# Four attention layers on one core: inputs turned by VectorE in blocks of 32, sums of exponentials on VectorE beside one layer, and both ends of a side layer placed last

## The chip, the cores and the metric

The kernel runs on one core of a Trainium2 chip. The metric is the device time of one execution in microseconds (us). The time before is the median of three runs. One more execution was taken by the hardware profiler, and all durations of single instructions come from that one.

The engines are called TensorE (PE in the profile, with its weight loads as PEld), VectorE (DVE), ScalarE (ACT), GpSimd (POOL) and SyncE (SP), which issues most DMAs.

## What is computed

The input x has 4 elements of 64x64 positions with 64 channels in float32. Four attention layers follow one another; every element goes through them alone. Cut to what matters:

```python
# layer 0: attention over all 4096 positions, normalised over j, summed over the queries
q, k, v = x @ Wq + bq, x @ Wk + bk, x @ Wv + bv          # each 4096 x 64
attn = softmax(q @ k.T, axis=-1)
x = gamma * (attn.T @ v) + x
# layer 1: 4096 queries with 8 channels, 1024 pooled keys, values with 32 channels
attn = softmax(theta(x) @ maxpool2(phi(x)).T)
x = x + sigma * ((attn @ maxpool2(g(x))) @ w_o + b_o)
# layers 2 and 3: group norm, then attention over all 4096 positions, projection, residual
w = softmax(q @ k.T / 8);  x = residual + (w @ v) @ Wp + bp
```

In layer 0 the factor 1/sum belongs to the row of the score matrix, and the rows are what the second product sums over. So the sum of a row's exponentials is needed before that product, and it is applied to the values.

## The kernel before, in words

**Stages and steps.** The fast path runs 12 attention stages one after another: layer 0 of elements 0 to 3 and layers 2 and 3 of each, mixed so that the small work between them always has a stage to run beside. A stage has 64 steps. `step` puts out, in this order, the two score tiles of the step with their exponentials (`first`, twice), and then the second products of an earlier step (`due`). The order of instructions on every engine is the order in which the Python code emits them; each engine works through its own list in order and waits on semaphores.

**Layer 0** (`layer0`). `first` writes a scores tile `s` of 128x1024 by four matmuls (L971), takes the exponential into a tile `p` (L975) and has ScalarE's accumulator sum each row into a column of `zs`. Every fourth tile completes a row block: VectorE adds the four columns (L977) and takes the reciprocal (L978). Three steps later `scale` multiplies the values by it on ScalarE (L985, `vs`), and `adds` forms the second product (L996).

**Layers 2 and 3** (`attention`). Scores are L1214, exponentials L1219, second products L1249. The sums are kept by VectorE, which adds every `p` to `zacc` (L1225).

**Tiles.** There are two scores tiles in PSUM, and everything that writes PSUM for a moment takes them in turn: scores, transposes, projections, sums. A matmul that needs one waits until the engine that read its last content is done. Accumulators have four tiles of their own. In SBUF there are 14 tiles for `p`.

**Side work.** `background` holds a generator, a chain of small pieces: layer 1 of an element, and what must be done before its next layer. Each `yield` names the place in a step where the next piece may go:
- MID: between the two second products of a step.
- ALONE: as MID, and no LATE piece in that step.
- LATE: in the middle of the second of these products.
- END: after all else.

A step grants pieces by a credit (`tempo`: 1.0 beside most of layer 0, 3.0 beside the stages that carry layer 1).

**Layer 1** (`layer1`). It runs as side work, over two halves j of the queries and 8 blocks k of the keys each. LATE gives two scores tiles (L1089) and their exponentials (L1095). VectorE adds these up (`accumulate`, L1104). With `bank` the second product stays in an accumulator; that is so for elements 1 to 3, beside layer 2. For element 0, beside layer 0 of element 1, there is no free accumulator (`bank` false): each second product (L1115, at END) goes to a scores tile, and VectorE adds it to `o` (L1124), the first one of each half being copied by ScalarE (L1126). `finish(j)` ends a half: row sums by TensorE (L1131), copied and summed by ScalarE (L1137), four reciprocals (L1140), a product (L1142), another sum on ScalarE for the range check (L1144), the output projection (L1150) and the addition to x (L1152). The end of half 0 is put between the scores of half 1, that of half 1 comes last.

**Inputs.** `load_x` loads an element in 8 DMAs of 32 partitions, each with pieces of 64 channels (256 bytes), positions on partitions. `transposed` turns it to channels on partitions: for each half, 8 TensorE transposes (L916) into a scores tile, copied out by VectorE (L862) or ScalarE (L870). This is the beginning of `before0`, which goes on with the projection (L883) and the values (L902, L903). Element 0 is loaded and transposed ahead of the first stage; elements 1, 2 and 3 as side work of stages 1, 3 and 5. Only element 1's copies are on VectorE.

**The end.** A flag, `bad`, counts partitions whose sums are out of range (L1776). After the last DMAs (L1516), all engines load it (L1793) and branch (L1794) around `general_path`, a slower form of the computation that is not run with these inputs.

Of the kernel before, what the change touches and what calls it, by code (L numbers as in the profile page):

```python
# [10 lines left out]
AF = mybir.ActivationFunctionType  # L11
ALU = mybir.AluOpType
AX = mybir.AxisListType
# [581 lines left out]
            layer3(layer2(layer1(layer0(here))), dst)  # L595


def fast_path(tc: tile.TileContext, a: dict, out: bass.AP, bad):

# [6 lines left out]
    nc = tc.nc  # L608
    x = a["x"]
# [162 lines left out]
    now = [0]  # L772
    due, before, urgent = {}, {}, []
    later = []
    back = {"gen": iter(()), "at": None, "credit": 0.0, "tempo": 1.0, "alone": -1}

    def background(tempo, *phases):
# [131 lines left out]
    def transposed(on, st):  # L909
        xin = st.pop("xin")  # L910
        xT = st["x"] = x_tile("xT")
        for g in range(2):
# [3 lines left out]
                nc.tensor.transpose(bank[i // 4][:, ds(i % 4 * P, P)], xin[:, g * 8 + i, :, :].rearrange("p i c -> p (i c)"), ident)  # L916
            evacuate(on, xT[:, wide(g)], s)

    def before0(on, st):
        yield from transposed(on, st)  # L920
        q = x_tile("q")
        yield from project(on, q, blocks[0][0], st["x"], blocks[0][1])
        st["q"] = q, swapped("q_swapped", q)
        st["v"] = x_tile("v").rearrange("p (j f) -> p j f", f=C)
        yield from values(st["v"], wv0, st["x"], bv0)
# [23 lines left out]
    def layer0(st):  # L949

        q, k, v = st.pop("q"), st["x"], st.pop("v")
        pairs = NB * NC // 2
        acc, ps, zs, scaled = {}, {}, {}, {}
        zsum, rz = check_columns(NB)

        def queries(m, i, e):

            c, n = divmod(m // 2, 4)
            return q[(c + i) % 2][half(i), ds(c // 2 * 1024 + m % 2 * 512 + n * P + e * C, C)]

        def first(u):
            m, c = divmod(u, NC)
            if c == 0:
                zs[m] = small.tile([P, NC], FP, tag="z0", name="z0")
            s = s_tile()
            for i in range(2):
                for e in range(2):  # L970
                    nc.tensor.matmul(  # L971
                        s[half(e), chunk(i)], queries(m, i, e), k[half(i), chunk(c)], start=True, stop=True
                    )
            p = ps[u] = p_tile()
            nc.scalar.activation(p, s, AF.Exp, accum_out=zs[m][:, c : c + 1])  # L975
            if c == NC - 1:
                nc.vector.tensor_reduce(zsum[:, m : m + 1], zs.pop(m), AX.X, ALU.add)  # L977
                nc.vector.reciprocal(rz[:, m : m + 1], zsum[:, m : m + 1])  # L978

        def scale(t):  # L980
            vs = scaled[t] = z_p.tile([P, C], FP, tag="vs", name="vs", bufs=1)
            for e in range(2):
                if 0 <= t - e < pairs:
                    m = 2 * (t - e) // NC
                    nc.scalar.activation(  # L985
                        vs[half(e), :], v[half(e), m, :], AF.Copy, scale=rz[half(e), m : m + 1]
                    )

        def add(t, e, n, vs, cols):

            if 0 <= t < pairs:
                m, c = divmod(2 * t + n, NC)
                if m == 0 and e == 0 and c not in acc:
                    acc[c] = acc_tile()
                for i in range(2):
                    nc.tensor.matmul(  # L996
                        acc[c][half(i), cols], vs[half(e), :], ps[2 * t + n][half(e), chunk(i)][:, cols],
                        start=(m == 0 and e == 0), stop=(m == NB - 1 and e == 1),
                    )
                    yield  # L1000

        def adds(t, n, within=None):
            for cols in parts(within, t * 2 < NC or t >= pairs - NC // 2):
                lower, upper = add(t, 0, n, scaled[t], cols), add(t - 1, 1, n, scaled[t], cols)
                for row_tile in (lower, upper) * 3:
                    next(row_tile, None)
            if n == 1:
                del scaled[t]
                for u in (2 * t - 2, 2 * t - 1):
                    ps.pop(u, None)  # L1010

        def finish(cs):
            xT = st["x"]
            for c in cs:
                nc.vector.scalar_tensor_tensor(xT[:, chunk(c)], acc.pop(c), gamma0, xT[:, chunk(c)], ALU.mult, ALU.add)
            if not acc:
                st["done0"] = True

        start = now[0]
        for t in range(pairs + 1):  # L1020
            g = start + t + 3
            before.setdefault(g, []).append(lambda t=t: scale(t))
            due.setdefault(g, []).extend([lambda *within, t=t, n=n: adds(t, n, *within) for n in range(2)])
        for g, cs in ((2, (0, 1)), (3, (2, 3))):
            due[start + pairs + g].append(lambda cs=cs: finish(cs))
        for t in range(pairs):
            step(lambda: (first(2 * t), first(2 * t + 1)))
        return start + pairs + 4


    def layer1(on, st, bank):
# [7 lines left out]
        s = s_tile()  # L1039
# [125 lines left out]
        for n in range(len(todo) + 1):  # L1165
            accumulate = None
            if n < len(todo):
                yield LATE
                accumulate = scores(*todo[n])
            if n:  # L1170
                if not bank:
                    yield END
                elif n == len(todo):
                    yield LATE
                add(*todo[n - 1])
            if accumulate and bank:
                later.append(accumulate)
            elif accumulate:
                accumulate()
            if n == NK:  # L1180
                end = finish(0)
                at = next(end)
            elif end is not None:
                yield at
                at = next(end, None)
                end = end if at is not None else None
        while end is not None:
            yield at
            at = next(end, None)
            end = end if at is not None else None  # L1190
        yield from finish(1)
        st["done1"] = True


# [273 lines left out]
    def layer3(st, not_before):  # L1468
# [12 lines left out]
        def final(acc, sums):  # L1481

            z = acc_tile()[:, 0:8]
            add_quarters(z, sums)
            z_columns, r_columns = check_columns(8)
            nc.vector.tensor_copy(z_columns, z)
            nc.vector.reciprocal(r_columns, z_columns)
            rest_in_range(z_columns, r_columns)
            r_columns = r_columns.rearrange("p (n i) -> p n i", n=4)
            t = o_p.tile([P, 2 * 4, C], FP, tag="turned", name="turned")  # L1490
            ks = slice((NC - 1) // 2 * 8, (NC - 1) // 2 * 8 + 8)
            turned = []
            for m in range(2):
                o, cols = o_tile("o")[:, 0:256], slice(m * 256, m * 256 + 256)
                nc.scalar.copy(o, acc[0][:, cols])
                nc.vector.tensor_tensor(o, o, acc[1][:, cols], ALU.add)
                s = s_tile()[:, 0:256]
                for n in range(2):
                    nc.tensor.matmul(s[:, ds(n * P, P)], o[:, ds(n * P, P)], wv3, start=True, stop=True)
                turned.append(s)  # L1500
            set_bad = count_bad()
            for m, s in enumerate(turned):
                n = slice(2 * m, 2 * m + 2)
                part = t.rearrange("p (i n) f -> p n i f", n=4)[:, n, :, :]
                nc.vector.tensor_tensor(
                    part, s.rearrange("p (n i f) -> p n i f", n=2, i=2),
                    r_columns[:, n, :].unsqueeze(3).to_broadcast([P, 2, 2, C]), ALU.mult,
                )
                nc.vector.tensor_tensor(
                    part, part, hb[:, ks, (NC - 1) % 2, :].rearrange("p (i n) f -> p n i f", n=4)[:, n, :, :], ALU.add  # L1510
                )
                if m == 0:
                    set_bad()
            for r in range(4):
                queue = nc.scalar if r % 2 else nc.sync
                queue.dma_start(dst[r, :, ks, (NC - 1) % 2, :], t[r * W2 : (r + 1) * W2, :, :])  # L1516
# [198 lines left out]

    def loads(st):
        yield MID
        load_x(st)


    background(1.0, rest(st0), second_half(s0, s0["v"]), pause(6), constants(), loads(s1), pause(6), before0("DVE", s1), loads(s2))
# [60 lines left out]
    assert not later  # L1782

    ctx.close()


def conv_seq_kernel(tc: tile.TileContext, a: dict, out: bass.AP):

    nc = tc.nc
    with tc.tile_pool(name="flag", bufs=1) as flag:  # L1790
        bad = flag.tile([1, 1], I32, name="bad")
        fast_path(tc, a, out, bad)
        n_bad = nc.values_load(bad[0:1, 0:1], min_val=0, max_val=128, skip_runtime_bounds_check_because="it is a count of 128 partitions")  # L1793
        with tc.If(n_bad > 0):  # L1794
            general_path(tc, a, out)

# [36 lines left out]
```

## Time and profile before

| what | value |
|---|---|
| median of 3 runs | 2997.26 us (2997.09 to 2997.95) |
| the profiled execution | 2997.72 us |
| its span, first to last instruction | 2996.0 us |
| granted TensorE clock | 0.999 |
| busy: TensorE, ScalarE, VectorE, GpSimd | 2971.6, 1939.1, 1759.2, 34.0 us |
| DMA | 25.79 MB in 42081 packets, 39872 of them under 512 bytes |
| TensorE transposes of inputs (L916) | 48 in side work, 16 ahead of the first stage |
| exponentials of layer 0 (L975) | 512, 1015 ns each, and 198 ns each to read the accumulator |

The page gives the busy time of every engine, the span in 40 slices, and the chain of work that ended last. Groups of instructions have a line number, the engine, the tiles written and read with their shapes, the count, the busy time with the mean of one, and the idle time of the engine ahead of them with what ended it. The waits name who waited for whom. The timeline lists instructions in order of time. A busy TensorE is not TensorE at its peak, as matmuls overlap and their ends are modelled; the distance between the first matmuls of two steps is a firmer measure.

### The profile page before, as it was taken

The numbers are of one execution on the slowest core, as the hardware profiler recorded it, in microseconds if no ns is written. First come the engines' busy times: TensorE is split into PE (matmuls) and PEld (weight loads), VectorE is DVE, ScalarE is ACT, GpSimd is POOL, SyncE is SP. The second block draws the span as 40 slices with busy tenths as digits, with TensorE's granted clock in tenths as the row PEclk, the third lists the DMA queues.
The fourth block names the chain that finished last, engine by engine and source line by source line (L and its number), as shares of the span: only waits on it lengthen the run. The fifth ranks groups of instructions, "written<-read, shape, count | busy, mean of one in ns | idle before, by whom it ended". The sixth has DMA issues, their size and how long they took to land.

```text
span 2996.0 us, 64727 instructions
## 1 busy us (share of the span) xinstructions
PE 2971.6 (99%) x28533; PEld 1128.5 (38%) x28533; DVE 1759.2 (59%) x2002; ACT 1939.1 (65%) x2813; POOL 34.0 (1%) x32
## 2 busy tenths in 40 slices
PE   9999999999999999999999999999999999999998
PEld 3333233333444433344443333333343334333333
DVE  1211332587731078762017887777877777877777
ACT  6877777665577866567886655655555655555554
POOL 0000000000000000000000000000000000000000
PEclk9999999999999999999999999999999999999999
DMA  2010000000001000000000000000000000000000
GB/s 37 2 29 5 1 1 1 19 2 12 4 1 29 1 5 1 15 2 15 2 2 5 2 15 1 19 5 8 5 19 9 15 2 1 16 8 5 8 5 9
DMA packets 42081, 25.79 MB, mean 9 GB/s; under 512 B 39872, under 2 KB 39872, under 8 KB 40384
## 3 DMA queue, kind: packets, MB, share of 16 engines
q1 hardware_dynamic: 40080, 21.17, 3.7%
q8 instruction: 225, 3.69, 0.5%
q10 hardware_dynamic: 1712, 0.41, 0.1%
q14 instruction: 64, 0.52, 0.1%
HBM read 4.79 MB, written 4.19 MB: 3 GB/s over the span
## 4 chain that ended last, share of the span: by engine, by line
PE 98%; ACT 1%; DVE 0%; issue 0%; DMA 0%; ACTq 0%; DVEq 0%
PE acc L1249 30%; PE s L1214 29%; PE s L971 15%; PE acc L996 15%; PE s L1089 2%; PE acc L1115 2%; ACT p L1095 1%; PE s L1115 1%; PE s L1277 1%; PE s L902 1%; PE s L1361 0%; PE s L883 0%; PE s L1275 0%; PE s L1458 0%; PE s L1150 0%; PE s L1061 0%
## 5 line engine op out<-in xcount | busy, mean ns | idle before, releaser
L1219 ACT ACTIVATE p<-s 128x1024 f32<-128x1024 f32 x1024 | 994.5, 1022 | 704.4 <-PE s L1214 695.0
L1225 DVE TENSOR_TENSOR zacc<-zacc,p 128x1024 f32<-128x1024 f32 x960 | 1174.0, 1223 | 361.7 <-ACT p L1219 320.2
L975 ACT ACTIVATE p<-s 128x1024 f32<-128x1024 f32 x512 | 519.5, 1015 | 43.3 <-PE s L971 24.3
L1249 PE MATMUL acc<-p,v 64*64 64x512 f32 (+1 forms) x4480 | 518.5, 556 | 0.0
L996 PE MATMUL acc<-p,vs 64*64 64x512 f32 (+1 forms) x4224 | 512.1, 578 | 0.5 <-ACT vs L985 0.5
L1249 PE MATMUL acc<-p,hT 64*64 64x512 f32 x4096 | 494.2, 590 | 0.0
L1214 PE MATMUL s<-q,k 64*64 64x512 f32 x2048 | 490.7, 590 | 1.7 <-ACT p L1095 1.7
L971 PE MATMUL s<-xT,q 64*64 64x512 f32 x2048 | 487.5, 591 | 2.5 <-DVE v L903 0.6
L971 PE MATMUL s<-xT,q_swapped 64*64 64x512 f32 x2048 | 488.5, 591 | 0.0
L1214 PE MATMUL s<-q,xT 64*64 64x512 f32 x2048 | 486.9, 589 | 0.0
L1214 PE MATMUL s<-q,h_swapped 64*64 64x512 f32 x2048 | 479.3, 589 | 0.0
L1214 PE MATMUL s<-q,k_swapped 64*64 64x512 f32 x2048 | 477.9, 590 | 0.2 <-DVE xT L1404 0.2
L977 DVE TENSOR_REDUCE all_z<-z 128x1 f32<-128x4 f32 x128 | 20.1, 157 | 632.6 <-ACT p L975 632.6
L1249 PEld LDWEIGHTS acc<-p,v 64*64 64x64 f32 x4480 | 174.4, 133 | 294.0 <-issue 291.8
L996 PEld LDWEIGHTS acc<-p,vs 64*64 64x64 f32 x4224 | 176.0, 133 | 270.8 <-issue 207.5
L985 ACT ACTIVATE vs<-v,all_r 64x64 f32<-64x64 f32 x512 | 176.6, 345 | 145.1 <-PE acc L996 72.0
L1249 PEld LDWEIGHTS acc<-p,hT 64*64 64x64 f32 x4096 | 156.7, 133 | 263.8 <-issue 263.1
L971 PEld LDWEIGHTS s<-xT,q_swapped 64*64 64x64 f32 x2048 | 146.0, 133 | 143.5 <-issue 113.1
L971 PEld LDWEIGHTS s<-xT,q 64*64 64x64 f32 x2048 | 146.0, 133 | 136.9 <-issue 109.2
L1214 PEld LDWEIGHTS s<-q,h_swapped 64*64 64x64 f32 x2048 | 144.0, 133 | 141.2 <-issue 135.4
L1214 PEld LDWEIGHTS s<-q,k_swapped 64*64 64x64 f32 x2048 | 143.9, 133 | 140.8 <-issue 97.4
L1214 PEld LDWEIGHTS s<-q,xT 64*64 64x64 f32 x2048 | 143.4, 133 | 140.1 <-issue 137.7
(233 smaller groups left out, 1552.4 us busy)
## 6 DMA issues: line engine op xcount, KB each, us to landing
k_swapped<-k SPq DMA_DIRECT2D x8, 512.0 KB, 6.0
h_swapped<-xT SPq DMA_DIRECT2D x8, 512.0 KB, 5.4
out_dram<-turned SPq DMA_DIRECT2D x62, 64.0 KB, 1.9
xin<-in_x_dram SPq DMA_DIRECT2D x24, 128.0 KB, 4.8
q_swapped<-q SPq DMA_DIRECT2D x6, 512.0 KB, 5.5
pg<-pg SPq DMA_DIRECT2D x8, 128.0 KB, 2.3
xin<-in_x_dram SPq DMA_DIRECT2D x12, 64.0 KB, 2.3
xin<-in_x_dram ACTq DMA_DIRECT2D x4, 64.0 KB, 2.7
```

The lines of the kernel that those rows point to most:

```text
L902: nc.tensor.matmul(s[:, ds(k * P, P)], rhs[:, ds((g * 8 + k) * P, P)], w, start=True, stop=True)
L971: nc.tensor.matmul(s[half(e), chunk(i)], queries(m, i, e), k[half(i), chunk(c)], start=True, stop=True)
L975: nc.scalar.activation(p, s, AF.Exp, accum_out=zs[m][:, c : c + 1])
L985: nc.scalar.activation(vs[half(e), :], v[half(e), m, :], AF.Copy, scale=rz[half(e), m : m + 1])
L996: nc.tensor.matmul(acc[c][half(i), cols], vs[half(e), :], ps[2 * t + n][half(e), chunk(i)][:, cols], start=(m == 0 and e == 0), stop=(m == ...
L1089: nc.tensor.matmul(ss[e][half(m), chunk(i)], pgs[0 if e == d else 1][r, ds(n * P + m * C, C)], th[r, chunk(i ^ j)], start=True, stop=True,)
L1095: nc.scalar.activation(pk[e], ss[e], AF.Exp)
L1115: nc.tensor.matmul(acc[quarter(q), :], g[:, k, :], ps[j, k][q // 2][:, chunk(q % 2)], start=(k == 0 or not bank), stop=(k == NK - 1 or not ...
L1214: nc.tensor.matmul(s[half(e), chunk(i)], k[(j + i) % 2][half(i), ds(j // 2 * P + e * C, C)], q[half(i), chunk(c)], start=True, stop=True,)
L1219: nc.scalar.activation(p, s, AF.Exp)
L1225: add = lambda: nc.vector.tensor_tensor(zaccs[c], p0, p, ALU.add)
L1249: nc.tensor.matmul(accs[c][e][half(i), cols], v[half(e), j, :], p[half(e), chunk(i)][:, cols], start=(j == 0), stop=(j == NB - 1),)
```

## The change

It has four parts.

1. Elements 1 to 3 are loaded by `load_blocks`: 4 DMAs of 32 partitions each, with pieces of 32 channels (128 bytes), so that each block of 32 positions by 32 channels lies where VectorE's 32x32 transpose can turn it in place. `transposed_blocks` does this with two VectorE instructions of 128x1024, from SBUF to SBUF. No TensorE work and no scores tile is used. The number of `yield`s is the same. Element 0 is loaded and transposed as before.
2. In `layer0`, while the side work stands at a LATE or END piece, that is beside the scores of layer 1 of element 0, the exponential is taken without ScalarE's accumulator, and VectorE sums the tile. That concerns 32 exponentials in 16 steps.
3. In `layer1` without `bank`, both ends come after all scores, and their pieces go in pairs: the two ALONE pieces in steps of their own, of the others one of each half in the same step.
4. The flag is loaded as soon as it is written, ahead of the last four DMAs; the branch stays where it was.

```diff
+    def load_blocks(st):
+        st["xin"] = t = x_tile("xin")
+        src = x[st["b"]].rearrange("h (i w) (q c) -> i q w h c", i=2, q=2)
+        for i in range(2):
+            for q in range(2):
+                nc.sync.dma_start(t[quarter(2 * i + q), :].rearrange("p (h c) -> p h c", c=32), src[i, q])
+
+    def transposed_blocks(st):
+        xin = st.pop("xin")
+        xT = st["x"] = x_tile("xT")
+        for g in range(2):
+            yield MID
+            nc.vector.transpose(xT[:, wide(g)], xin[:, wide(g)])
...
     def before0(on, st):
-        yield from transposed(on, st)
+        yield from transposed_blocks(st)
...
-            nc.scalar.activation(p, s, AF.Exp, accum_out=zs[m][:, c : c + 1])
+            z = zs[m][:, c : c + 1]
+            if back["at"] in (LATE, END):
+                nc.scalar.activation(p, s, AF.Exp)
+                nc.vector.tensor_reduce(z, p, AX.X, ALU.add)
+            else:
+                nc.scalar.activation(p, s, AF.Exp, accum_out=z)
...
-            if n == NK:
+            if n == NK and bank:
                 end = finish(0)
...
-        yield from finish(1)
+        if bank:
+            yield from finish(1)
+        else:
+            ends = [finish(j) for j in range(2)]
+            at = [next(end) for end in ends]
+            while at[0] is not None:
+                if at[0] == ALONE:
+                    yield ALONE
+                    at[0] = next(ends[0], None)
+                yield at[1]
+                at = [at[0] if at[0] != at[1] else next(ends[0], None), next(ends[1], None)]
...
                 if m == 0:
                     set_bad()
+            flag.append(read_flag())
             for r in range(4):
                 queue = nc.scalar if r % 2 else nc.sync
...
     def loads(st):
         yield MID
-        load_x(st)
+        load_blocks(st)
```

More of the change, by code (lines that the diff above doesn't have):

```diff
@@ L595, in general_path, with fast_path @@
             layer3(layer2(layer1(layer0(here))), dst)
-def fast_path(tc: tile.TileContext, a: dict, out: bass.AP, bad):
+def fast_path(tc: tile.TileContext, a: dict, out: bass.AP, bad, read_flag):
     nc = tc.nc
@@ L774, in fast_path @@
     later = []
+    flag = []
     back = {"gen": iter(()), "at": None, "credit": 0.0, "tempo": 1.0, "alone": -1}
@@ L1784, in fast_path @@
     ctx.close()
+    return flag[0]
 def conv_seq_kernel(tc: tile.TileContext, a: dict, out: bass.AP):
@@ L1791, in conv_seq_kernel @@
         bad = flag.tile([1, 1], I32, name="bad")
-        fast_path(tc, a, out, bad)
-        n_bad = nc.values_load(bad[0:1, 0:1], min_val=0, max_val=128, skip_runtime_bounds_check_because="it is a count of 128 partitions")
+        n_bad = fast_path(tc, a, out, bad, lambda: nc.values_load(
+            bad[0:1, 0:1], min_val=0, max_val=128, skip_runtime_bounds_check_because="it is a count of 128 partitions"
+        ))
         with tc.If(n_bad > 0):
```

## The prediction

> **What bounds the kernel now.** I read the page's busy times and its chain first. The program has 12 attention stages of 64 steps each (4 of layer 0, 8 of layers 2 and 3).
>
> ```profile
> PE 2971.6 (99%) x28533; PEld 1128.5 (38%) x28533; DVE 1759.2 (59%) x2002; ACT 1939.1 (65%) x2813; POOL 34.0 (1%) x32
> PE 98%; ACT 1%; DVE 0%; issue 0%; DMA 0%; ACTq 0%; DVEq 0%
> ```
>
> TensorE is busy throughout and is 98% of the chain that ended last. Only two things can pay: TensorE work that disappears, and TensorE waits that disappear. Work moved between ScalarE and VectorE pays only where one of them releases TensorE late. So I measured steps in the timeline, as the distance from one step's first score matmul to the next. An undisturbed step is 3.43 us: 768 such steps would be 2634 us, and the rest is prologue, tail and the side work of layers 1 to 3.
>
> The second view is TensorE's timeline where element 1 is transposed (start, duration, then what runs), and two rows of the busy times by stretch (length, then busy time and count of PE, weight loads, DVE, ACT, POOL).
>
> ```profile
> 146.47 1.04 PE L996 MATMUL acc<-p,vs 64*64 64x512 f32 x8
> 147.43 1.09 PE L916 MATMUL s<-ident,xin 128*128 128x128 f32 x8
> 148.46 1.09 PE L996 MATMUL acc<-p,vs 64*64 64x512 f32 x8
> ...
> 137.88:144.75 6.87, 6.87 (x69) 2.45 (x64) 0.32 (x2) 5.84 (x12) 0.00 (x0) 1.00 0.00 0
> 144.75:153.98 9.23, 9.23 (x84) 3.96 (x80) 2.35 (x4) 5.84 (x12) 0.00 (x0) 1.00 0.01 2
> ...
> 1233.03:1242.29 9.26, 9.26 (x84) 4.03 (x80) 6.57 (x6) 5.69 (x6) 0.00 (x0) 1.00 0.00 0
> ```
>
> Eight transposes stand in the middle of a step and TensorE does nothing else for that time. Two ordinary steps take 6.87 us, the two with transposes 9.23 us, and for element 3 (beside layer 2) 9.26 us.
>
> The third view is the waits between 294 and 412 us: layer 1 of element 0 beside layer 0 of element 1, where most of the rest of the change lies (engine, line, releaser: total, times, longest).
>
> ```profile
> PE s L1115 <- ACT p L1095: 8.0, 15, 0.5
> ACT p L1095 <- PE s L1089: 19.3, 16, 1.2
> ACT p L975 <- PE s L971: 10.2, 14, 1.2
> DVE o L1124 <- PE s L1115: 44.8, 14, 7.4
> ```
>
> TensorE loses 0.53 us in each of 15 steps before L1115, because its scores tile is released by layer 1's exponential (L1095). That exponential itself waits 1.2 us for TensorE's L1089. ScalarE is ahead of TensorE here, not behind. The rows of the two stretches below show such steps in full: 6.68 us long, TensorE 6.15, VectorE 3.28 or 2.96, ScalarE 4.74.
>
> ```profile
> 315.84:322.52 6.68, 6.15 (x69) 1.81 (x65) 3.28 (x5) 4.74 (x9) 0.00 (x0) 1.00 0.01 2
> 322.52:329.19 6.67, 6.14 (x68) 1.80 (x64) 2.96 (x3) 4.73 (x9) 0.00 (x0) 1.00 0.01 4
> ```
>
> **What the Trainium skill says.** "VectorE: DVE Perf Modes", section "The three transpose paths": VectorE turns 32x32 blocks only and writes to SBUF, while TensorE's full transpose lands in PSUM. The trace agrees: L916 needs a copy out (L862, L870), L1233 does not. The same page, "Rules for kernel authors", calls `tensor_reduce` the slowest VectorE operation, always at single rate. L1419 below, the shape that the change adds, takes 1212 ns, no slower here than a tensor_tensor of that size (1223 ns). "DMA: Bandwidth & Descriptors", section "Why small descriptors are slow (HBM only)", warns of pieces of 256 bytes and less. Both layouts of x are there (256 bytes before, 128 after), and no load of 128-byte pieces is in this trace. The same page, "Latency and other measured facts", gives a `tensor_load` about 600 ns; the trace has 492 to 725 ns.
>
> The prices that I use, from the groups (busy, mean ns | idle before):
>
> ```profile
> L1233 DVE STREAM_TRANSPOSE p<-zacc 128x1024 f32<-128x1024 f32 x32 | 39.8, 1245 | 2.7
> L1419 DVE TENSOR_REDUCE stat<-xT 128x1 f32<-128x1024 f32 x8 | 9.7, 1212 | 0.0
> L1140 DVE RECIPROCAL r<-r 128x128 f32<-128x128 f32 x32 | 30.0, 940 | 0.8 <-ACT r L1137 0.8
> L975 ACT ACTIVATION_READ_ACCUMULATOR p<-s 128x1 f32 x512 | 101.2, 198 | 2.9
> L1144 ACT ACTIVATE r<-r 128x512 f32<-128x512 f32 x8 | 5.0, 628 | 0.0
> ```
>
> **Part 1, the inputs of elements 1 to 3.** Removed: 48 TensorE transposes, 6 uses of a scores tile and 6 evacuations (2 on VectorE, 4 on ScalarE at 1.01 us). Added: 6 VectorE transposes at 1.245 us. TensorE gains 9.23 - 6.87 = 2.36 for element 1 and 9.26 - 6.87 = 2.39 for element 3; with the same for element 2, **-7.15 us**.
> - Element 1: VectorE exchanges a 1.225 us copy for a 1.245 us transpose, in steps where it works 1.2 us or less. Hidden.
> - Elements 2 and 3: VectorE has 2.45 us a step there (two L1225), so 3.7 in a step of 3.43. It falls behind by 0.27 us in each of two steps. The projection that reads the first half is two steps later, and its own steps (4.29 us) let VectorE catch up. Hidden.
> - Loads: 24 issues on SP become 12 of twice the size. Element 1's are issued at 39 us and needed near 147; they took 9 us in all. Even four times that is hidden, and elements 2 and 3 wait far longer. On SP only later exchanges of tiles are behind them.
>
> **Part 2, 32 exponentials summed by VectorE** (16 steps, those whose side work stands at layer 1's scores). ScalarE loses 32 accumulator reads of 0.2 us. As it waits for TensorE in the steady steps, that brings nothing. In the two steps after layer 1's first evacuation on ScalarE (7.00 and 6.88 us long) its lateness costs TensorE about 0.2 us each: **-0.4** (0 to -0.5). VectorE gains 2 x 1.21 us a step: L1124 0.69, two L1104 2.35, two sums 2.42, every second step 0.33 for L977 and L978. That is 5.8 us in a step of 6.68. L1124 releases the scores tile that TensorE needs 0.86 us later, so it must not be late; 0.9 us remain. Its order on VectorE is: sums, L977, L978, L1124, then L1104.
>
> The exception is the last of these steps, which has only L1115 and no new scores. It is 4.61 us long:
>
> ```profile
> 400.69 0.69 DVE L1124 TENSOR_TENSOR o<-o,s 128x512 f32<-128x512 f32 x1 [2.44 <-PE s L1115]
> 401.29 2.35 DVE L1104 TENSOR_TENSOR zacc<-zacc,p 128x1024 f32<-128x1024 f32 x2
> 405.30 0.69 DVE L1124 TENSOR_TENSOR o<-o,s 128x512 f32<-128x512 f32 x1 [1.65 <-PE s L1115]
> ```
>
> VectorE is free at 403.65. Now it has 2.42 + 0.33 us to do before the last L1124, which therefore starts near 406.4 instead of 405.30. Its tile is the next step's second scores tile, which TensorE wanted at 406.0 and would get at 407.1: **+1.05 us** (0.7 to 1.3). Who is late next is the second exponential of that step, once.
>
> **Part 3, both ends of layer 1 last.** TensorE's work is the same and so is the number of steps: 16 of scores, one last addition and 11 without, where before two of the end's pieces stood between the scores. A step with L1131 took 4.64 between scores and 4.59 after them: **-0.05**. Two reciprocals a step (1.88 us) fit VectorE, which has little beside layer 0. The two L1144 with their reads now fall into one step: 2 x (0.63 + 0.1) = 1.45 us on ScalarE, which idles 0.38 us a step there. A single one delayed its next exponential by 0.14 us, two will by about 0.85, and TensorE has 0.7 us to spare: **+0.15** (0 to 0.7). The preparation of layer 2 behind it moves up by one step, with the same shapes.
>
> **Part 4, the flag read ahead of the last store.** The flag is written at 2989.15, the stores were issued at 2989.97. The five reads took 492 to 725 ns, so they end by 2989.9 if they start at once. On SP and ACT the last two stores each are queued behind the read. The end is set by the last landing at 2994.2 and SP's waits after it, and the reads were beside that flight: 0. The final waits may come in a better order: **-0.2** (-0.3 to +0.2).
>
> **Sum.** -7.15 - 0.4 + 1.05 - 0.05 + 0.15 - 0.2 = -6.6 us. The profiled execution took 2997.72 (span 2996.0 and 1.7 around it), which would become 2991.1. Against the median of 2997.26, 0.46 lower, it is **2990.6**. A measurement of this kernel can tell about 0.2%, 6.0 us, from no change, so the line is at 2991.3 and this case is close to it.
>
> **The rivals.**
> - *ScalarE's relief pays.* If the 0.53 us waits at L1115 went because the exponentials come earlier, 15 x 0.5 = 8 us more: 2983. Against it: L1095 waits for L1089. 0.07.
> - *VectorE's lateness eats part.* If the two L1144, the late L1124, or a backlog beside layer 2 (two transposes and layer 1's L1152 within three steps) cost 1 to 3 us more than summed, 2991.5 to 2993.5: within the bound. For it: VectorE has only 0.9 us to spare in 16 steps. 0.25.
> - *VectorE becomes the bound beside layer 0: slower.* L1124 sits behind the two sums. Once VectorE's work exceeds the step, 6.68 us, every one of 16 steps is longer. That happens when a sum takes over 1.65 us instead of 1.21; at double, 2.42, the work is 8.2 and the cost 16 x 1.5 = 24 us, so 3014. Against it: the row for the same shape. 0.08.
> - *The loads in 128-byte pieces come late.* Element 1 would have to take over 100 us instead of 9, with VectorE and the sums behind it on hold. 0.01.
>
> **How the numbers follow.** The main case has 0.59, of which I put about 0.53 beyond the line and 0.06 within it, as its bounds run from -7.7 to -5.6. With the first rival, faster has 0.60; with the second, no change 0.31; slower 0.09. The range of 2989.2 to 2993.0 covers the main case's bounds and most of the second rival; the first and third lie outside.
>
> **What would show it.** Right: no L916 after the prologue; steps of 3.43 us at the six places; steps of 6.68 us beside layer 1 with VectorE busy about 5.7; one TensorE wait of about 1 us for L1124's successor at the last of them; the L1115 waits unchanged. Wrong: steps beyond 6.7 us there, or waits of TensorE for the sums or the transposes.

## The result and the profile after

| | median | runs | lowest to highest |
|---|---|---|---|
| before | 2997.18 us | 8 | 2994.02 to 2999.58 |
| after | 2987.16 us | 8 | 2984.41 to 2987.83 |

The ratio is 0.9967, with a 95% interval of 0.9956 to 0.9978. The change saves 10.0 us where 6.6 were forecast. The direction was right. The time lies 2.0 us below the range, so the gain was underestimated.

The profiled execution of after took 2984.41 us, with a span of 2982.6. Of the 13.4 us between the two spans, 3.29 lie ahead of the first scores of stage 1 (13.20 us into the span before, 9.91 after). They are not the change's, as the last section shows. From the first scores on the difference is 10.1 us, which agrees with the medians. I read it by stage (first score matmul of a stage to that of the next):

| stage | before | after | difference | forecast |
|---|---|---|---|---|
| 1 (inputs of element 1) | 239.48 | 236.87 | -2.61 | -2.36 |
| 2 (layer 1 of element 0) | 288.69 | 286.52 | **-2.17** | **+0.75** |
| 3 (inputs of element 2) | 280.27 | 277.91 | -2.36 | -2.4 |
| 5 (inputs of element 3) | 280.60 | 277.78 | -2.81 | -2.39 |
| the eight others, with the tail | | | -0.13 | -0.2 |

Stage 2 holds nearly the whole error: 2.9 of some 3.4 us. Of stage 1's difference 0.23 lie in its first step (4.46 against 4.23 us), which follows the same slow start of the kernel, and of stage 5's some 0.3 in a step whose cause stays open.

The page of after, busy times, chain, and the loads of x (transfers, KB each, median us to landing):

```profile
PE 2957.3 (99%) x28485; PEld 1125.8 (38%) x28485; DVE 1799.4 (60%) x2038; ACT 1932.2 (65%) x2777; POOL 34.0 (1%) x32
PE 98%; ACT 1%; DVE 1%; issue 0%; DMA 0%; ACTq 0%; DVEq 0%
xin<-in_x_dram SPq DMA_DIRECT2D x12, 256.0 KB, 6.4
```

TensorE has lost 48 instructions, the transposes, and still sets the end.

The busy times of after by stretch (length, then PE, weight loads, DVE, ACT, POOL). First two pairs of ordinary steps where the inputs of elements 1 and 3 are turned, then two steps beside layer 1, then the step after the last scores:

```profile
141.22:148.08 6.86, 6.86 (x68) 2.44 (x64) 2.69 (x4) 5.83 (x12) 0.00 (x0) 1.00 0.01 2
1222.58:1229.44 6.86, 6.86 (x68) 2.84 (x64) 6.34 (x6) 3.88 (x4) 0.00 (x0) 1.00 0.01 2
...
309.24:315.69 6.45, 5.89 (x69) 1.62 (x65) 5.54 (x7) 4.57 (x7) 0.00 (x0) 1.00 0.01 3
315.69:322.14 6.45, 5.89 (x69) 1.63 (x66) 5.21 (x5) 4.57 (x7) 0.00 (x0) 1.00 0.00 0
...
391.50:397.05 5.55, 4.87 (x44) 1.24 (x44) 1.65 (x4) 3.03 (x6) 0.00 (x0) 1.00 0.00 0
```

The 9.23 and 9.26 us of before have become 6.86. Beside layer 1 the step is 6.45 us where I had said that it stays at 6.68. VectorE works 5.2 or 5.5 us in it (forecast 5.7). The wait that the first rival had named as the place for a gain has not moved. The waits of after between 294 and 412 us (total, times, longest; L1137 and L1117 are the old L1115 and L1095, L1111 the old L1089, L987 the old L971, L1146 the old L1124):

```profile
PE s L1137 <- ACT p L1117: 8.3, 15, 0.6
ACT p L1117 <- PE s L1111: 19.0, 15, 1.3
PE s L987 <- DVE o L1146: 0.7, 1, 0.7
```

TensorE still waits 0.55 us in each of 15 steps for layer 1's exponential, and that still waits 1.3 us for TensorE. The third line is the new wait, once, as forecast.

The groups of after for what was added (busy, mean ns | idle before): the sums, the transposes, the exponentials without and the reads with the accumulator:

```profile
L995 DVE TENSOR_REDUCE z<-p 128x1 f32<-128x1024 f32 x32 | 37.4, 1212 | 8.2 <-ACT p L994 8.2
L933 DVE STREAM_TRANSPOSE xT<-xin 128x1024 f32<-128x1024 f32 x6 | 7.3, 1234 | 0.0
L994 ACT ACTIVATE p<-s 128x1024 f32<-128x1024 f32 x32 | 31.0, 1022 | 7.2 <-PE s L987 7.1
L997 ACT ACTIVATION_READ_ACCUMULATOR p<-s 128x1 f32 x480 | 94.9, 198 | 2.7
```

The prices were right: 1212 ns for a sum (1212 forecast) and 1234 for a transpose (1245). What was wrong is where ScalarE's relief goes.

**Where the 0.23 us of a step come from.** ScalarE's timeline in one step beside layer 1, before:

```profile
310.32 1.02 ACT L975 ACTIVATE p<-s 128x1024 f32<-128x1024 f32 x1 [0.70 <-PE s L971]
311.35 0.20 ACT L975 ACTIVATION_READ_ACCUMULATOR p<-s 128x1 f32 x1
311.46 1.01 ACT L975 ACTIVATE p<-s 128x1024 f32<-128x1024 f32 x1
312.37 0.19 ACT L975 ACTIVATION_READ_ACCUMULATOR p<-s 128x1 f32 x1
313.77 1.94 ACT L1095 ACTIVATE p<-s 128x1024 f32<-128x1024 f32 x2 [1.21 <-PE s L1089]
```

and the same step after:

```profile
310.39 1.94 ACT L994 ACTIVATE p<-s 128x1024 f32<-128x1024 f32 x2 [0.55 <-PE s L987]
313.61 1.94 ACT L1117 ACTIVATE p<-s 128x1024 f32<-128x1024 f32 x2 [1.28 <-PE s L1111]
```

From the start of the first exponential to the end of the last instruction on the scores, ScalarE took 2.24 us before (310.32 to 312.56) and 1.94 after. The 0.30 us matter because of what layer 1's scores wait for. The instructions of L1089 before, 312.2 to 313.8 us (count: duration ns min/median/max, first and last start):

```profile
L1089 PEld LDWEIGHTS s<-th,pg x16: 127/130/132, 312.4 to 312.7; 8*64 8x64 f32 x16
L1089 PE MATMUL s<-th,pg x16: 587/613/639, 312.4 to 313.1; 8*64 8x512 f32 x16
```

and of the same group after, L1111:

```profile
L1111 PEld LDWEIGHTS s<-th,pg x16: 127/130/132, 312.4 to 312.5; 8*64 8x64 f32 x16
L1111 PE MATMUL s<-th,pg x16: 587/612/639, 312.4 to 313.0; 8*64 8x512 f32 x16
```

These 16 matmuls write two scores tiles in turn. TensorE's timeline has the group as one row, before and after, and the part of the weight loads of before that runs after 312.56 us:

```profile
312.35 1.36 PE L1089 MATMUL s<-th,pg 8*64 8x512 f32 x16
312.42 1.11 PE L1111 MATMUL s<-th,pg 8*64 8x512 f32 x16
...
312.61 0.22 PEld L1089 LDWEIGHTS s<-th,pg 8*64 8x64 f32 x12
```

The first weight load for the second tile started 0.26 us after the group's first in before (312.61 against 312.35), and starts 0.01 us after it in after. 312.61 is 0.05 us after the second accumulator read ended, and the trace has this load waiting for the semaphore that ScalarE raised at the end of that read: the read gave the tile free. This wait is in no waits table, because matmuls for the first tile run meanwhile and TensorE counts as busy. It shows only in these starts and in the group's length: 1.36 us before, 1.11 after. The Trainium skill, "Perfetto Trace Analysis", section "Identifying the Most-Contended Engine", says that the busy share of matmuls is not a good measure of how near TensorE is to its limit, because pipelined instructions look smaller in a trace. This trace agrees on the measure, but by the opposite error: the overlap hid a wait as busy time, and TensorE's busy time in the step fell from 6.15 to 5.89 us with the same matmuls.

### The profile page after: what moved, and what is told of

Read it like the earlier page. It is cut to its first block, busy times and chain, and to the rows that moved or that the text cites. A ratio compares the mean times of both kernels' runs of the same rounds, so it can differ in the third digit from the quotient of the medians.

```text
span 2982.6 us, 64616 instructions
## 1 busy us (share of the span) xinstructions
PE 2957.3 (99%) x28485; PEld 1125.8 (38%) x28485; DVE 1799.4 (60%) x2038; ACT 1932.2 (65%) x2777; POOL 34.0 (1%) x32
## 4 chain that ended last, share of the span: by engine, by line
PE 98%; ACT 1%; DVE 1%; issue 0%; DMA 0%; ACTq 0%; DVEq 0%
PE acc L1281 30%; PE s L1246 30%; PE s L987 15%; PE acc L1018 15%; PE s L1111 2%; PE acc L1137 2%; ACT p L1117 1%; PE s L1309 1%; PE s L1137 1%; PE s L903 1%; PE s L1393 0%; PE s L884 0%; PE s L1307 0%; PE s L1490 0%; PE s L1413 0%; PE s L1172 0%
## 5 line engine op out<-in xcount | busy, mean ns | idle before, releaser
L1251 ACT ACTIVATE p<-s 128x1024 f32<-128x1024 f32 x1024 | 994.4, 1022 | 706.4 <-PE s L1246 698.3
L997 ACT ACTIVATE p<-s 128x1024 f32<-128x1024 f32 x480 | 486.9, 1015 | 34.7 <-PE s L987 15.9
L987 PE MATMUL s<-xT,q 64*64 64x512 f32 x2048 | 487.9, 591 | 2.5 <-DVE v L904 0.6
L987 PE MATMUL s<-xT,q_swapped 64*64 64x512 f32 x2048 | 488.6, 591 | 0.7 <-DVE o L1146 0.7
L987 PEld LDWEIGHTS s<-xT,q_swapped 64*64 64x64 f32 x2048 | 146.1, 133 | 144.0 <-issue 113.7
L987 PEld LDWEIGHTS s<-xT,q 64*64 64x64 f32 x2048 | 147.2, 133 | 135.1 <-issue 105.8
```

The costliest lines, as they stand in the source:

```text
L987: nc.tensor.matmul(s[half(e), chunk(i)], queries(m, i, e), k[half(i), chunk(c)], start=True, stop=True)
L997: nc.scalar.activation(p, s, AF.Exp, accum_out=z)
L1251: nc.scalar.activation(p, s, AF.Exp)
```

## The experiments

My theory after the result (theory A in what follows): the steps beside layer 1 are shorter because ScalarE, without the two accumulator reads, gives layer 1's second scores tile free earlier. The rivals: the reads cost TensorE nothing, as predicted, and another part of the change shortens the steps (the order of the ends, which is theory B, or the transposes that take no scores tile), or it is the work given to VectorE that matters. First each part alone, added to the kernel before.

**Part 1 alone** (only `load_blocks` and `transposed_blocks`):

> Part 1 alone. Both theories: the six steps that held transposes shrink to 3.43 us, stages 1, 3 and 5 are 2.4 us shorter each (7.1 us together), and the steps of layer 1 beside layer 0 stay at 6.68 us. If the blocks also disturb something (late loads, VectorE behind beside layer 2), the gain of a stage is below 2.2 us.

Measured: 2989.45 us against 2996.81, ratio 0.9974 (0.9964 to 0.9984). Stages 1, 3 and 5 fell by 2.38, 2.38 and 2.76, and stage 2 did not change (288.69). Part 1 has no hand in the shorter steps. Of the 2.76, some 0.3 also came in stage 5 of the next two kernels, which lack part 1. It is a single step of 3.82 us before that is 3.53 and 3.54 there; its cause stays open. Against the stage 5 of those two, part 1 is worth 2.4 there too.

**Part 2 alone** (in `layer0` of before):

```diff
+            if back["at"] in (LATE, END):
+                nc.scalar.activation(p, s, AF.Exp)
+                nc.vector.tensor_reduce(z, p, AX.X, ALU.add)
```

> Part 2 alone, the ends of layer 1 still in between. There the side work stands at MID or ALONE when half 1's steps begin, so only about 9 steps get VectorE's sums. Theory A (the reads of ScalarE's accumulator release the second scores tile late, and TensorE's L1089 waits for it): those steps take 6.45 us, the others stay at 6.68; stage 2 is about 2.3 us shorter. Theory B (the prediction's: the reads cost TensorE nothing, and the gain of the whole change in these steps came with the order of the ends): all stay at 6.68, stage 2 within 0.5 us.

Measured: 2994.42 us, ratio 0.9993 (0.9984 to 1.0002), which by itself can't be told from no change. The stages tell more: stage 2 took 286.43 us, 2.26 less, and no other stage moved by more than 0.3. The busy times of one of its steps:

```profile
308.44:314.89 6.45, 5.89 (x69) 1.63 (x65) 5.21 (x5) 4.57 (x7) 0.00 (x0) 1.00 0.00 0
```

So part 2 makes the 6.45. It does so only in the first half's steps here: once half 0's end stands between the scores, the side work stands at MID or ALONE when a step begins, the condition is false, and the steps go back to 6.68.

**Part 3 alone** (`if n == NK and bank`, and the paired ends):

> Part 3 alone: ends last, accumulators kept on ScalarE. Theory A: the steps of layer 1 stay at 6.68 us, no wait for the last L1124, stage 2 within 0.3 us of before. Theory B: the steps shrink to 6.45 us and stage 2 gets about 3 us shorter.

Measured: 2997.2 us, ratio 1.0 (0.9991 to 1.0009). Stage 2 grew by 0.33 us, where up to 0.3 was expected. Its steady step, in the same columns:

```profile
309.02:315.70 6.68, 6.15 (x68) 1.81 (x64) 2.96 (x3) 4.74 (x9) 0.00 (x0) 1.00 0.00 0
```

The order of the ends does not shorten a step. Most of its 0.33 is a step of 6.88 us where before had 6.62. It follows the second half's first addition, which ScalarE copies (L1126 of before), and the light step of half 0's end used to lie between. What part 3 does is to let part 2 cover the second half.

**Part 4 alone** (`flag.append(read_flag())` moved up):

> Part 4 alone. The prediction has -0.2 us for SP's waits at the end. By the two profiles, the last landing comes 0.4 us later after the last matmul and SP is done 0.4 us sooner after it: 0.0 us. Either way the total cannot be told from before; the profile's tail can.

Measured: 2996.8 us, ratio 0.9999 (0.9991 to 1.0008). The reads on the two engines that issue the stores, SyncE and ScalarE, took 0.48 us, from 2988.79, and the last stores were issued at 2989.58, 0.3 us after these ended. Nothing waited for the reads, and nothing was gained.

Then the reason for the 6.45, by changes to the kernel after. **Only one exponential of each step without its accumulator**, the first (`u % 2 == 0` added to the condition) or the second (`u % 2 == 1`):

> The whole change, but in the 16 steps VectorE sums only the first exponential of each step; the second keeps ScalarE's accumulator. Theory A with both reads in the release (the first exponential's read of 0.21 us delays the second, and the second's own read ends 0.09 us after it): of TensorE's 0.26 us wait 0.05 stay, steps of 6.47 to 6.50 us; at the last step VectorE has one sum less and L1146's equivalent starts in time, so the step after it is 4.6 us instead of 5.55. If only the second's own read holds the tile: 6.6 us. Theory B: 6.68.

> The mirror image: VectorE sums only the second exponential of each step, the first keeps its accumulator. Theory A: the first read still delays the second exponential by 0.21 us, only the second's own read (0.09 us) is gone: steps of 6.58 to 6.60 us. If the second's read alone held the tile: 6.45. The step after the last addition is 4.6 us as in the run with the first exponential.

Measured: 2988.19 and 2988.1 us against 2997.09 (ratios 0.997, 0.9958 to 0.9981, and 0.9966, 0.9951 to 0.998). The step after the last scores took 4.66 and 4.77 us, where 4.6 was expected in both. The steady step is 6.59 us in both. For the second this was expected; for the first 6.47 to 6.50 was, and that is a miss. ScalarE's timeline shows why. The first exponential without its read:

```profile
307.49 1.03 ACT L994 ACTIVATE p<-s 128x1024 f32<-128x1024 f32 x1 [0.70 <-PE s L987]
308.41 1.02 ACT L997 ACTIVATE p<-s 128x1024 f32<-128x1024 f32 x1
309.44 0.20 ACT L997 ACTIVATION_READ_ACCUMULATOR p<-s 128x1 f32 x1
```

and the second without its read:

```profile
307.43 1.03 ACT L997 ACTIVATE p<-s 128x1024 f32<-128x1024 f32 x1 [0.70 <-PE s L987]
308.47 0.20 ACT L997 ACTIVATION_READ_ACCUMULATOR p<-s 128x1 f32 x1
308.58 1.01 ACT L994 ACTIVATE p<-s 128x1024 f32<-128x1024 f32 x1
```

In these steps a read that follows the step's first read starts 0.10 us before its exponential ends (312.37 against 312.47 in before). A single read starts 0.01 us after it, at either place; why stays open. So the chain is 2.24 us with both reads, 2.15 or 2.16 with one, 1.94 with none. The step is 6.68, 6.59, 6.45. The first 0.09 us go to the step in full, of the next 0.21 only 0.14 do: with no read left, the second tile's weight loads follow the first tile's at once, and an earlier release has nothing more to give there.

**Both the accumulator and VectorE's sum** (its result to a spare column):

```diff
+            nc.scalar.activation(p, s, AF.Exp, accum_out=z)
             if back["at"] in (LATE, END):
+                spare = small.tile([P, 1], FP, tag="spare", name="spare")
+                nc.vector.tensor_reduce(spare, p, AX.X, ALU.add)
```

> The whole change, but the 32 exponentials keep ScalarE's accumulator, and VectorE's sums are taken as well, into spare columns that nothing reads. Theory A: steps of 6.68 us as before, since the reads are back, and the late addition after the last of them stays (a step of 5.5 us in place of 4.6). If VectorE's work by itself were what shortened the steps, 6.45.

Measured in one run: 2991.0 us, steps of 6.68, the step after the last scores 5.42. One steady step:

```profile
313.52:320.20 6.68, 6.15 (x68) 1.81 (x64) 5.44 (x7) 4.74 (x9) 0.00 (x0) 1.00 0.01 2
```

**Neither of them** (GpSimd writes a constant in place of the sums):

```diff
-                nc.vector.tensor_reduce(z, p, AX.X, ALU.add)
+                nc.gpsimd.memset(z, 1e29)
```

> The whole change, but these 32 exponentials are summed by nobody: neither accumulator nor VectorE; GpSimd writes a constant into the columns, so the output is not the reference's. Theory A: steps of 6.45 us, and no late addition after the last, a step of 4.6 us: VectorE's sums cost that one wait (0.94 us) and nothing else, so stage 2 is 285.5 us against 286.5 with the whole change. If VectorE's sums also cost in the steps, these are below 6.4.

Measured in one run: 2986.32 us, steps of 6.45 but for two of 6.52, the step after the last scores 4.66. One steady step:

```profile
312.32:318.77 6.45, 5.89 (x68) 1.63 (x64) 3.19 (x5) 4.57 (x7) 0.20 (x4) 1.00 0.01 3
```

With the kernel after (sums without reads: 6.45 and 5.55) and part 3 alone (reads without sums: 6.68 and 4.66) the two make a full cross: the reads decide the steady step whether VectorE sums or not, and the sums decide the step after the last scores, whether ScalarE reads or not.

**Each sum twice:**

```diff
-                nc.vector.tensor_reduce(z, p, AX.X, ALU.add)
+                for _ in range(2):
+                    nc.vector.tensor_reduce(z, p, AX.X, ALU.add)
```

> The whole change with each of the 32 sums taken twice by VectorE: the prediction's third rival made true. VectorE's work is then 5.5 + 2.4 = 8.0 us in a step of 6.45, L1124's equivalent comes late in every step and TensorE waits for it: 15 or 16 steps of 7.9 to 8.2 us, stage 2 some 22 to 28 us longer than with single sums. If VectorE's lateness is absorbed, the steps stay near 6.45.

Measured in one run: 3008.09 us. Stage 2 took 307.61 us, 21.1 more than after, where 22 to 28 were expected. Twelve of its steps took 7.29 to 8.01 us (15 or 16 of 7.9 to 8.2 were expected). One of them and the step after the last scores, and then TensorE's waits for the addition between 300 and 425 us:

```profile
313.62:321.25 7.63, 6.10 (x68) 1.62 (x65) 7.56 (x8) 4.68 (x7) 0.00 (x0) 1.00 0.01 2
411.60:421.35 9.75, 6.56 (x44) 1.56 (x44) 4.11 (x6) 3.03 (x6) 0.00 (x0) 0.82 0.00 0
```

```profile
PE s L987 <- DVE o L1147: 17.3, 14, 3.2
```

VectorE is busy for 7.56 of 7.63 us and TensorE waits for its addition in 14 steps: the third rival, made real. Not all of the 21.1 us is waiting. In the second row the granted clock is 0.82: after TensorE's longest wait, 3.19 us, the trace records half the clock for 3.41 us. This step is 4.21 us longer than in after, 2.51 from the longer wait and some 1.7 from the slow clock, so that the sums by themselves cost about 19.4.

**The last two sums left to ScalarE.** The late step comes from the two sums ahead of the last addition. After's VectorE timeline (start, duration, then what runs):

```profile
387.63 2.36 DVE L1126 TENSOR_TENSOR zacc<-zacc,p 128x1024 f32<-128x1024 f32 x2
389.90 2.34 DVE L995 TENSOR_REDUCE z<-p 128x1 f32<-128x1024 f32 x2
392.27 0.16 DVE L999 TENSOR_REDUCE all_z<-z 128x1 f32<-128x4 f32 x1
392.47 0.17 DVE L1000 RECIPROCAL all_r<-all_z 128x1 f32<-128x1 f32 x1
392.55 0.67 DVE L1146 TENSOR_TENSOR o<-o,s 128x512 f32<-128x512 f32 x1
```

The addition (L1146) has two sums and the row block's reciprocal ahead of it, as forecast. In that step the side work stands at END, so the condition can be cut:

```diff
-            if back["at"] in (LATE, END):
+            if back["at"] == LATE:
```

> The whole change, with VectorE's sums only while the side work stands at LATE: 15 steps instead of 16, so that the last of them, which has no new scores of layer 1, keeps ScalarE's accumulators. Theory A: steps of 6.45 us stay, VectorE is free for the last L1124 in time, the step after it is 4.65 us instead of 5.55; stage 2 near 285.7 us, 0.9 less than with the whole change, 2986.3 us in all. If the late addition had another cause: no difference.

It ran beside the kernel after on one chip:

> The changed kernel as it is, beside the one with 15 steps on the same chip: 2987.2 us as before, 0.9 us above the other by theory A.

Measured: 2985.58 us (2985.38 to 2986.43, 5 runs), ratio 0.9964 (0.9951 to 0.9978) against the kernel before. The kernel after took 2986.98 there (2983.34 to 2987.33, 6 runs), 0.9967 (0.9955 to 0.9979). The steady steps are 6.45 in both, the step after the last scores 4.66 and 5.56. Stage 2 is 0.9 us shorter (285.64 against 286.55). The stage shows the gain. The whole times, whose intervals overlap, can't tell it.

```profile
393.94:398.61 4.67, 4.67 (x45) 1.24 (x44) 0.69 (x1) 2.92 (x6) 0.00 (x0) 1.00 0.00 0
```

In this stretch of that kernel TensorE has no gap, and VectorE has only the addition.

## Why the prediction fell short

- **Part 1, right.** Forecast -7.15 us. Alone it gave -2.38 in each of its stages, -7.1 together, with the open step of stage 5 set aside, and the whole kernel was 7.4 faster. VectorE, the scores tiles and the loads hid what they were said to hide. Element 1's loads took 10.9 us from the first issue to the last landing (45.3 to 51.3 us landed, 9.2 in all before) and were needed 90 us later. The Trainium skill, "DMA: Bandwidth & Descriptors", section "Why small descriptors are slow (HBM only)", fits in direction: half the piece, 1.2 times the time for the same bytes. The number of DMAs was halved too, so this does not show that the pieces are the cause.
- **Part 2, the step that failed.** "As it waits for TensorE in the steady steps, that brings nothing." I read this off ScalarE's 1.2 us wait for L1089. But L1089 was itself waiting for ScalarE's previous read, inside a group that counts as busy. ScalarE and TensorE release each other twice in a step, and a wait of one does not prove that it is ahead at the other place. The twelve steady steps that the kernel after and part 3 alone share fell by 0.23 each, 2.74 us together where I had 0.
- **The steps after the first additions on ScalarE, about right.** Forecast -0.4 for two steps. They fell by 0.30 and 0.17. The second half's, which part 3 brings up, fell by another 0.17.
- **The late last addition, right.** Forecast +1.05. The step after the last scores is 5.55 us against 4.66 in part 3 alone, +0.89. The 0.7 us wait in the table is the shown part of it.
- **Part 3, right in kind.** Forecast +0.10 in all. The two L1144 in one step cost about 0.05 instead of 0.15. Unforecast was the late step of the second half, so that part 3 alone cost stage 2 0.33.
- **Part 4.** Forecast -0.2, measured nothing above the noise. My own base value was 0, and the -0.2 for "a better order" had no row behind it. I also gave the page's 600 ns for a `tensor_load` as its time, where the page calls it a floor; reads of 492 ns before and 0.48 us here are below it.

For stage 2 the sum becomes +0.33 (part 3) - 2.74 - 0.64 + 0.89 = -2.16; measured -2.17.

Of the rivals, the first was closest and yet wrong in its place. ScalarE's relief did pay, but not at the L1115 waits. These stayed (8.0 and 8.3 us), as both ends of that wait moved up together. Its size was 0.23 a step and not 0.5. The second did not happen: the late addition cost 0.89, less than the 1.05 in the sum, and only part 3's late step was unforecast. The third is where I said, once the work of VectorE passes the step: with doubled sums 21 us, 19.4 without the slow clock, 24 forecast. The fourth did not happen.

The list of signs pointed to the fault at once: "steps of 6.68 us" was wrong and "the L1115 waits unchanged" was right. Together they point to a release that the waits table does not list. Its signs of being wrong, though, were all of slower steps; none was for a gain that I had missed.

## What to carry to other kernels

When two engines hand tiles back and forth, follow every hand-over of a step in both directions before calling relief of one of them free; a wait of engine A for B says nothing about the place where B waits for A. A group of matmuls that writes several tiles can wait for one of them while it counts as busy: compare its length, and the starts of its weight loads, with those of an undisturbed group. And a sum moved to another engine stands in that engine's queue: here it delayed the last addition by 0.9 us, and leaving the last step's two sums on the accumulator took that back.

## What the runs showed of the hardware

- **An accumulator read is not worth its duration.** It lasts 198 ns. Taking away one of two was worth 0.09 us at the release of the tile, taking away both 0.30, as in these steps the second read overlaps the end of its exponential by 0.10 us and a single one does not.
- **A long wait of TensorE came with a slow clock behind it, once.** With doubled sums the wait of 3.19 us was followed by 3.41 us at half the granted clock, and the score matmuls of 64x512 there took 1.06 to 1.11 us, against 0.59 to 0.64 in the same place of after. Between the first scores and the tail, the next longest wait of that kernel, 1.35 us, and those of the other traces, all under 1 us, had no such drop behind them. It is one case, and the cause isn't shown.
- **The prologue varies by 3 us between executions, together with the start of the full clock.** The groups of the same 16 matmuls of 64x512, before:

```profile
L883 PE MATMUL acc<-xT,A 64*64 64x512 f32 x16 | 3.7, 1071 | 0.0
```

and after:

```profile
L884 PE MATMUL acc<-xT,A 64*64 64x512 f32 x16 | 1.9, 602 | 0.0
```

With the same prologue code as after, the kernels of the single exponentials and of the last two sums began their first scores at 12.3 to 12.9 us, and the repeat of after at 9.71. So it goes with the execution, not with the change. The clock column reads 1.00 for both prologues, but it takes a stretch without a clock record for full clock. The trace of before has its first record of full clock at 13.56 us, just after these matmuls (9.7 to 13.4 us); that of after has it at 5.21, ahead of them (8.0 to 9.9 us). All 13 kept traces follow this order: a mean of 602 ns where the record starts by 5.3 us (two traces), 855 at 11.4 (one), 1002 to 1048 between 12.4 and 12.9 (three), 1071 from 13.1 on (seven). The Trainium skill, "TensorE: Matmul & The Clock Gate", section "Part 1: The HAM clock gate (the "warmup" mystery)", says that the count and the duration of slow matmuls at the start vary from run to run of one kernel. These traces agree, with 602 to 1071 ns; what sets the start of the full clock isn't shown.
